# The input laid out by tiles, and Toeplitz blocks loaded in eighths over twelve groups

## The chip, the cores and the metric

The kernel runs on one core of a Trainium2 chip. The metric is the device time of one execution in microseconds. Before the change the median of three runs is 941.27 us (940.22 to 941.31).

## The reference

Two layers follow each other on x of shape 4 x 64 x 256 x 256 in float32. The first is a long two-dimensional convolution whose filter is separable: each channel has a filter hx along the rows and hy along the columns, both from a small network of sines.

```python
hx = _implicit_filter(z, Xw1, Xb1, Xw2, Xb2, Xw3, Xb3, Xwo, Xfreq, t, deltas)
hy = _implicit_filter(z, Yw1, Yb1, Yw2, Yb2, Yw3, Yb3, Ywo, Yfreq, t, deltas)
k = jnp.transpose(jnp.einsum('ijk,imk->ijmk', hx, hy)[0], (2, 0, 1))
k_f = jnp.fft.rfft2(k, s=(fft_size, fft_size)) / fft_size
u_f = jnp.fft.rfft2(x, s=(fft_size, fft_size))
y = jnp.fft.irfft2(u_f * k_f, s=(fft_size, fft_size))[..., :L, :L]
out = y + x * bias[:, None, None]
```

The second layer whitens the 64 channels: a mean and a covariance from every ninth pixel, five Newton-Schulz steps for its inverse square root, and a product with all pixels.

```python
x1_s = x1[:, ::STRIDE ** 2]
mean1 = jnp.mean(x1_s, axis=-1, keepdims=True)
cov = x1_s @ x1_s.T / x1_s.shape[1] + EPS * jnp.eye(B)
deconv = _isqrt_newton_schulz(cov, N_ITER)
out = deconv @ (x1 - mean1)
```

## The kernel before

**The start.** The filters are computed first (lines 134 to 163): four small matmuls deep, with sines on ScalarE and range reduction on VectorE between them. The result, `taps`, has 128 rows (64 channels of each of the two filters, f = 0 and f = 1) and 384 columns. It is stored to DRAM as `g_d` (line 166), and the two rows that the first channels need also as `g0_d` (line 165).

**Toeplitz blocks.** A convolution along one axis is a product with a Toeplitz matrix. `load_toeplitz` (line 173) makes that matrix by a DMA that reads `g_d` at addresses overlapping by one element from partition to partition. One set `toep[g]` serves a group g of eight channels: 128 partitions (two halves of 64), two filters, eight channels and 256 columns. There are eight sets, and two buffers for them. One call of `load_toeplitz` loads one half of the partitions of one filter, for all eight channels: 64 x 8 pieces of 1 KB, 512 KB. Four calls make a set.

**The main loop.** `steps` has 32 pairs (g, n): eight channel groups g, and for each the four images n. A step has four groups of work (`group`, line 302), each on two channels: c = 0, 2, 4, 6. So one g has sixteen groups, here counted as k = 4n + c/2. A group multiplies the two channels of x with the f = 0 Toeplitz blocks, which gives `o1`, and in the same stretch multiplies the `o1` made two groups earlier with the f = 1 blocks. `toeplitz_products` (line 185) splits both into blocks of 64 rows, so that one product runs on the upper and the other on the lower half of TensorE's rows at once. Each pair of 64-row block and filter half uses only the columns from its own offset on: line 208 takes `t[parts, : stop : -1]` with `stop = HP * k - 1`. For f = 0 the second half of the partitions (64 to 127) serves the odd blocks, and for f = 1 the first half does; odd blocks never use the first 64 columns.

**What follows a product.** ScalarE copies the first product to `o1` (line 320). VectorE adds x times the bias to the second and writes `y` (line 325), and it picks the sampled pixels for the covariance (line 249). SP stores y for the two channels to DRAM, `y_d` (line 339).

**The order on SP's queue.** The order of all engines in the main loop is that of the program text. SP issues, in each group: the store of y; then one load of x for two channels (`load_x`, line 103, 512 KB) of the step after next; then, in the four groups from c = 2 of n = 1 to c = 0 of n = 2, one quarter of the next Toeplitz set (lines 379 to 383). The store of y waits for VectorE, and what stands behind it on SP waits too. In x's place in DRAM a row of 256 pixels is 1 KB, and a tile's partition p takes the rows p and 128 + p of a channel, so that a load of x has 512 pieces of 1 KB.

**Before the loop.** SP issues the eight loads of x for the first two steps, then the store to `g0_d`, and then eight loads for `toep[0]` (lines 353 to 355): two channels of it first, from `g0_d`, and then the other six.

**The end.** From the step before the last on, SP reads y back in pieces of 2 MB (`yi`, line 287). After the covariance and the inverse root, TensorE multiplies, ScalarE and VectorE add the shift (lines 511 and 514), and GpSimd issues the stores of the output (line 519).

Of the kernel before, what the change touches and what calls it, by code (L numbers as in the profile page):

```python
# [44 lines left out]
NB, C, L = 4, 64, 256  # L45
P, H2 = 128, 2
EMB, ORDER = 33, 64
PIX = L * L
CG = 8
HP = P // 2  # L50
# [5 lines left out]
GW = P + L  # L56
# [9 lines left out]
def conv_whiten_kernel(ctx: ExitStack, tc: tile.TileContext, a: dict, out: bass.AP):  # L66
    nc = tc.nc
    x = a["x"]
# [28 lines left out]
    bias = const.tile([P, C], F32, tag="bias", name="bias")  # L97
    nc.scalar.dma_start(out=bias, in_=a["bias"].partition_broadcast(P))

    def new_x(g, n):  # L100
        return big.tile([P, CG, H2, L], F32, tag="in", name=f"x_{g}_{n}")

    def load_x(t, g, n, c):
        nc.sync.dma_start(
            out=t[:, c : c + 2].rearrange("p c b w -> p (c b) w"),
            in_=x[n, g * CG + c : g * CG + c + 2].rearrange("c (b p) w -> p (c b) w", p=P),
        )

    steps = [(g, n) for g in range(C // CG) for n in range(NB)]
    loaded = {s: new_x(*s) for s in steps[:2]}  # L110
    for step, t in loaded.items():
        for c in range(0, CG, 2):
            load_x(t, *step, c)

    ident = const.tile([P, P], F32, tag="ident", name="ident")
    make_identity(nc, ident)
# [1 line left out]
    for n in range(NB):  # L118
        t = spool.tile([P, FP], F32, tag="samp", name=f"samp{n}")
# [24 lines left out]
    for i in range(3):  # L144
        for u in range(2):
            pm = psA.tile([P, P], F32, tag="psA", name=f"pm{i}_{u}")
            nc.tensor.matmul(pm, lhsT=wt, rhs=hs[u], start=True, stop=True)  # L147
            half = slice(u * P, (u + 1) * P)
            arg, k, nxt = (scratch[:, 2 + 3 * i + v, half] for v in range(3))
# [9 lines left out]
    for u in range(2):  # L159
        half = slice(u * P, (u + 1) * P)  # L160
# [7 lines left out]
    def new_toeplitz(g):  # L168


        return tpool.tile([P, 2, CG, L], F32, tag="toep", name=f"toep_{g}")

    def load_toeplitz(t, g, f, half, lo=0, hi=CG):
        source, row = (g0_d, 2 * f) if g == 0 and hi == 2 else (g_d, f * C + g * CG + lo)
        nc.sync.dma_start(
            out=t[half * HP : (half + 1) * HP, f, lo:hi],
            in_=bass.AP(
                tensor=source.tensor,
                offset=source.offset + row * GW,
                ap=[[1, HP], [GW, hi - lo], [1, L]],  # L180
            ),
        )

# [41 lines left out]
    def pack_by_pe(g, n, yt, cs):  # L225

        pk = psA.tile([P, H2, cs.stop - cs.start, NJ], F32, tag="psA", name=f"pk_{cs.start}")
        for s in range(STEP):
            for b in range(H2):
                nj = (L - s + STEP - 1) // STEP  # L230
                nc.tensor.matmul(  # L231
                    pk[:, b, :, 0:nj],
                    lhsT=pick[:, (s - b) % STEP, :],
                    rhs=yt[:, cs, b, s : s + STEP * (nj - 1) + 1 : STEP],
                    start=(s == 0 and b == 0),
                    stop=(s == STEP - 1 and b == H2 - 1),
                    skip_group_check=True,
                )
        dst = samp[n][:, :, :, g * CG + cs.start : g * CG + cs.stop]
        nc.scalar.copy(dst[:, 0], pk[:, 0].rearrange("p c j -> p j c"))  # L240
        nc.vector.tensor_copy(dst[:, 1], pk[:, 1].rearrange("p c j -> p j c"))  # L241
# [15 lines left out]
    def covariance(n):  # L257

        pc = psA.tile([P, C + 1], F32, tag="psA", name=f"pc{n}")
        for b in range(H2):  # L260
            for j in range(NJ):
                half = slice(C * (j % 2), C * (j % 2 + 1))
                nc.tensor.matmul(  # L263
                    pc[half],
                    lhsT=samp[n][:, b, j, 0:C],
                    rhs=samp[n][:, b, j, :],
                    start=(b == 0 and j < 2),
                    stop=(b == H2 - 1 and j >= NJ - 2),
                    skip_group_check=True,
                )  # L270
        nc.vector.scalar_tensor_tensor(cov, pc, 1.0 / NSAMP, cov, ALU.mult, ALU.add)  # L271
# [18 lines left out]
    def load_next():  # L290
        loaded[len(loaded)] = load_y(len(loaded))

    loaded_x, loaded = loaded, {}
# [3 lines left out]
    def bank(name):  # L297
        return psA.tile([P, H2, L], F32, tag="psA", name=name)

    orders = [list(range(L // HP)), list(reversed(range(L // HP)))]  # L300

    def group(first, second):
# [46 lines left out]
    with tc.manual_schedule(  # L349
        engines={engines.PE, engines.SP, engines.DVE, engines.Activation, engines.Pool}  # L350
    ):
        toep = {0: new_toeplitz(0)}
        for lo, hi in ((0, 2), (2, CG)):
            for part in range(4):
                load_toeplitz(toep[0], 0, part // 2, part % 2, lo, hi)
        for i, (g, n) in enumerate(steps):
            xt = loaded_x.pop((g, n))
            yt = big.tile([P, CG, H2, L], F32, tag="out", name=f"y_{g}_{n}")
            for c in range(0, CG, 2):
                item = (g, n, c, xt, yt, [])  # L360
                if g == C // CG - 1 and n > 1 and c == 4:
                    covariance(n - 2)
                group(item, pending.pop(0) if len(pending) == 2 else None)
                pending.append(item)
                if i == 0 and c == 6:

                    fold = const.tile([P, C], F32, tag="fold", name="fold")
                    nc.vector.tensor_tensor(fold, ident[:, 0:C], ident[:, C:P], ALU.add)
                    twice = const.tile([C, 2, C], F32, tag="twice", name="twice")
                    for u in range(2):  # L370
                        nc.vector.tensor_copy(twice[:, u], ident[0:C, 0:C])

                part = (c - 2) // 2 % 4
                to = i + 2 if c else i + 1
                if to < len(steps) and to > 1:
                    if part == 0:
                        loaded_x[steps[to]] = new_x(*steps[to])
                    load_x(loaded_x[steps[to]], *steps[to], 2 * part)
                tg, tn = steps[i if c else i - 1]
                if tn == 1 and tg + 1 < C // CG and (i or c):  # L380
                    if part == 0:
                        toep[tg + 1] = new_toeplitz(tg + 1)
                    load_toeplitz(toep[tg + 1], tg + 1, part // 2, part % 2)
                if i + 2 >= len(steps) and c > 0:
                    for _ in range(2 if i + 2 == len(steps) and c == 2 else 1):
                        load_next()

        g, n, c, xt, yt, _ = pending[0]
        group(None, pending[0])
        pack_by_pe(g, n, yt, slice(0, CG // 2))  # L390
        group(None, pending[1])
        covariance(NB - 2)
        pack_by_pe(g, n, yt, slice(CG // 2, CG))
        covariance(NB - 1)
        while len(loaded) < len(homes):
            load_next()
# [3 lines left out]
    for i in range(2):  # L400
        t = o1pool.tile([P, H2 * L], F32, tag="o1", name=f"chain{i}")
# [90 lines left out]
    for i, (v, q) in enumerate(pieces):  # L492
# [3 lines left out]
        part = FP if 1 < i < len(pieces) - 2 else FP // 4  # L496
# [42 lines left out]
def _laid_out(inputs):  # L539

    import numpy as np

    def of(name):
        return [np.asarray(inputs[f"L0_conv_{f}{name}"]) for f in "XY"]

    zw = np.concatenate([np.asarray(inputs["L0_conv_z"])[0, ::-1].T] + of("w1"), axis=1)
    cols = np.stack([np.concatenate(of(k), axis=-1).reshape(P) for k in ("b1", "b2", "b3", "freq")], 1)
    wbd = np.zeros((P, 3, P), np.float32)
    for i, k in enumerate(("w2", "w3", "wo")):
        for f, w in enumerate(of(k)):  # L550
            wbd[f * ORDER : (f + 1) * ORDER, i, f * ORDER : (f + 1) * ORDER] = w
    return {"zw": zw, "cols": cols, "wbd": wbd.reshape(P, 3 * P)}
# [23 lines left out]
```

## Time and profile before

| | us |
|---|---|
| median of the runs | 941.27 |
| profiled execution | 938.56 |
| its span, first to last instruction | 936.8 |
| PE busy | 796.7 (85%) |
| PE weight loads busy | 639.0 (68%) |
| DVE busy | 649.5 (69%) |
| ACT busy | 480.7 (51%) |
| POOL busy | 31.7 (3%) |

The mean granted TensorE clock is 0.956. The page's last part lists the DMAs, with the median time from issue to landing:

```profile
x<-in_x_dram SPq DMA_DIRECT2D x128, 512.0 KB, 5.5
y_d<-y SPq DMA_DIRECT2D x128, 512.0 KB, 3.7
yi<-y_d SPq DMA_DIRECT2D x32, 2048.0 KB, 16.5
out_dram<-yi POOLq DMA_DIRECT2D x28, 2048.0 KB, 43.1
toep<-g_d SPq DMA_DIRECT2D x28, 512.0 KB, 10.3
```

PE is TensorE, DVE is VectorE, ACT is ScalarE, POOL is GpSimd and SP is the sync engine, which issues most of the DMAs. PEld is TensorE's loading of stationary operands, which overlaps its matmuls. The share of a DMA row is the mean busy share of the core's 16 DMA engines; it can read somewhat over 1. In the windows that follow, times are counted from the start of the span.

### The profile page before, as it was taken

To read this page: it belongs to the slowest core of one execution; us is meant where nothing else is said; L and a number is where in the kernel's file an instruction comes from. 1 tells how busy PE (TensorE), PEld (TensorE's weight loads), DVE (VectorE), ACT (ScalarE), POOL (GpSimd) and SP (SyncE) were. 2 spreads that over 40 slices of the span, in tenths; PEclk is the share of its full clock that TensorE was granted. 3 is DMA by queue.
4 is the path that set the end of the run, shared out by engine and by line. 5 is a ranking of instruction groups with operands and counts; after the bars stand their busy time and mean duration, and the time that the engine had idled before them with its cause. 6 is when DMAs were issued, how large, how long until landed. Compare 5 with 4: busy or idle time off the path is not lost.

```text
span 936.8 us, 27864 instructions
## 1 busy us (share of the span) xinstructions
PE 796.7 (85%) x11850; PEld 639.0 (68%) x11850; DVE 649.5 (69%) x861; ACT 480.7 (51%) x792; POOL 31.7 (3%) x71
## 2 busy tenths in 40 slices
PE   2999999999999999999999999999687777766400
PEld 2899999999999999899999999989421111111100
DVE  3058687778768786778687768662399999996600
ACT  2245454544445454445454545330299888876500
POOL 3000000000000000000000000000020000000010
PEclk9999999999999999999999999999799999998755
DMA  7499789779879879879979977899999999999998
GB/s 230 111 250 305 236 243 294 239 232 267 284 231 284 267 229 277 263 234 259 278 231 249 293 233 226 289 395 362 415 362 420 428 431 428 430 429 431 430 431 356
DMA packets 164112, 287.67 MB, mean 307 GB/s; under 512 B 6384, under 2 KB 154261, under 8 KB 156309
## 3 DMA queue, kind: packets, MB, share of 16 engines
q1 hardware_dynamic: 156784, 218.18, 72.3%
q0 software_dynamic: 6336, 67.11, 16.9%
q8 instruction: 94, 1.54, 0.7%
q10 hardware_dynamic: 868, 0.60, 0.2%
q14 instruction: 30, 0.24, 0.1%
HBM read 151.44 MB, written 134.42 MB: 305 GB/s over the span
## 4 chain that ended last, share of the span: by engine, by line
PE 69%; issue 15%; DVE 13%; DMA 1%; ACT 1%; POOL 0%; POOLq 0%; ACTq 0%; DVEq 0%; SPq 0%
PE p L205 65%; DVE yi L514 12%; PE pk L231 2%; PE pc L263 2%; POOL out_dram L519 0%; PE po L506 0%; DMA toep<-g_d 0%; DMA g_d<-scratch 0%; PE ZY L421 0%; DVE scratch L154 0%; PE YT L421 0%; PE pm L147 0%; DVE scratch L151 0%; ACT scratch L150 0%; ACT L439 0%
## 5 line engine op out<-in xcount | busy, mean ns | idle before, releaser
L205 PE MATMUL p<-toep,x 64*64 64x64 f32 (+3 forms) x5120 | 595.6, 287 | 8.0 <-DMA toep<-g_d 6.1
L205 PE MATMUL p<-toep,o 64*64 64x64 f32 (+3 forms) x5120 | 589.3, 285 | 1.3 <-issue 1.2
L205 PEld LDWEIGHTS p<-toep,x 64*128 64x128 f32 (+1 forms) x5120 | 546.3, 168 | 34.0 <-DMA toep<-g_d 6.3
L205 PEld LDWEIGHTS p<-toep,o 64*128 64x128 f32 (+1 forms) x5120 | 542.0, 166 | 13.7 <-issue 2.0
L320 ACT COPY o<-p 64x512 f32<-64x512 f32 x512 | 296.8, 580 | 318.3 <-PE p L205 310.7
L325 DVE SCALAR_TENSOR_TENSOR y<-x,bias,p 128x512 f32<-128x512 f32 x256 | 180.6, 743 | 169.1 <-PE p L205 168.2
L249 DVE COPY_PREDICATED samp<-mask,y 128x448 f32<-128x448 int32 (+1 forms) x279 | 275.5, 988 | 6.4
L514 DVE TENSOR_SCALAR yi<-po,shift 64x512 f32<-64x512 f32 x256 | 192.1, 750 | 22.5 <-PE po L506 15.9
L506 PE MATMUL po<-yi,W 64*64 64x512 f32 x1024 | 150.0, 654 | 62.6 <-DVE yi L514 41.3
L511 ACT ACTIVATE yi<-po,shift 64x512 f32<-64x512 f32 x256 | 174.8, 683 | 41.9 <-PE po L506 34.7
L506 PEld LDWEIGHTS po<-yi,W 64*64 64x64 f32 x1024 | 35.4, 141 | 176.3 <-DVE yi L514 128.7
L519 POOL DMA_DIRECT2D out_dram<-yi x44 | 23.6, 537 | 270.5 <-DMA out_dram<-yi 108.8
L405 POOL MEMSET chain<- 64x64 f32 x1 | 0.1, 144 | 618.6 <-PE p L205 618.6
L263 PEld LDWEIGHTS pc<-samp 128*64 128x64 f32 x464 | 14.3, 137 | 1.7 <-ACT samp L240 0.7
L231 PE MATMUL pk<-y,pick 128*128 128x112 f32 (+1 forms) x72 | 15.3, 386 | 0.0
L263 PE MATMUL pc<-samp 128*64 128x65 f32 x464 | 14.9, 223 | 0.4 <-ACT samp L240 0.4
L231 PEld LDWEIGHTS pk<-y,pick 128*128 128x128 f32 x72 | 14.5, 207 | 0.2
L240 ACT COPY samp<-pk 128x116 f32<-128x116 f32 x2 | 0.5, 270 | 25.8 <-PE pk L231 15.3
L147 PE MATMUL pm<-scratch 128*128 128x128 f32 (+1 forms) x12 | 3.8, 474 | 8.7 <-ACT scratch L156 6.2
L271 DVE SCALAR_TENSOR_TENSOR cov<-pc,cov 128x65 f32<-128x65 f32 x4 | 0.9, 228 | 12.1 <-PE pc L263 12.1
L147 PEld LDWEIGHTS pm<-scratch 128*128 128x128 f32 (+1 forms) x12 | 2.9, 313 | 9.4 <-ACT scratch L156 6.8
L241 DVE COPY samp<-pk 128x116 f32<-128x116 f32 x2 | 0.6, 279 | 11.4 <-ACT samp L240 11.4
(71 smaller groups left out, 46.7 us busy)
## 6 DMA issues: line engine op xcount, KB each, us to landing
x<-in_x_dram SPq DMA_DIRECT2D x128, 512.0 KB, 5.5
y_d<-y SPq DMA_DIRECT2D x128, 512.0 KB, 3.7
yi<-y_d SPq DMA_DIRECT2D x32, 2048.0 KB, 16.5
out_dram<-yi POOLq DMA_DIRECT2D x28, 2048.0 KB, 43.1
toep<-g_d SPq DMA_DIRECT2D x28, 512.0 KB, 10.3
out_dram<-yi POOLq DMA_DIRECT2D x16, 512.0 KB, 10.0
toep<-g_d SPq DMA_DIRECT2D x4, 384.0 KB, 7.6
toep<-g_d SPq DMA_DIRECT2D x4, 128.0 KB, 3.1
```

The source lines that it names most:

```text
L147: nc.tensor.matmul(pm, lhsT=wt, rhs=hs[u], start=True, stop=True)
L205: mm = nc.tensor.matmul(ps[q : q + w, m, HP * k : L], lhsT=src[parts, k // 2, m * P + q : m * P + q + w], rhs=t[parts, : stop : -1] if k e ...
L231: nc.tensor.matmul(pk[:, b, :, 0:nj], lhsT=pick[:, (s - b) % STEP, :], rhs=yt[:, cs, b, s : s + STEP * (nj - 1) + 1 : STEP], start=(s == 0 ...
L249: nc.vector.copy_predicated(dst, m, src)
L263: nc.tensor.matmul(pc[half], lhsT=samp[n][:, b, j, 0:C], rhs=samp[n][:, b, j, :], start=(b == 0 and j < 2), stop=(b == H2 - 1 and j >= NJ ...
L271: nc.vector.scalar_tensor_tensor(cov, pc, 1.0 / NSAMP, cov, ALU.mult, ALU.add)
L320: nc.scalar.copy(o1[to], units[u][0][0][fr])
L325: nc.vector.scalar_tensor_tensor(yt[:, c + u], xt[:, c + u], bias[:, ch : ch + 1], units[u][1][0], ALU.mult, ALU.add,)
L506: nc.tensor.matmul(po[u][halves[k]], lhsT=W[halves[u]], rhs=yt[halves[u], cols[k]], start=True, stop=True,)
L511: nc.scalar.activation(yt[halves[0], cols[k]], po[0][halves[k]], AF.Identity, bias=shift[halves[k]])
L514: nc.vector.tensor_scalar(yt[halves[1], cols[k]], po[1][halves[k]], shift[halves[k]], None, ALU.add)
L519: nc.gpsimd.dma_start(out=o[:, end - part : end], in_=yt[:, end - part : end])
```

## The change

The change has four parts.

1. The host hands x over in the order of the tiles: image, channel group, partition, channel, row half, pixel. A load of x then reads 4 KB that lie together for each partition, 128 pieces instead of 512.
2. Before the loop only the first step's x is loaded. The four loads of the second step's x are issued behind the eight loads of `toep[0]`.
3. The next Toeplitz set is loaded in eighths (four channels instead of eight), in the groups k = 2, 3, 5, 6, 8, 10, 11 and 13 of the g before it. The first set keeps its eight loads.
4. In half of the Toeplitz loads (where filter and half differ) the first 64 columns, which no product reads, are left out: 768 B in a piece instead of 1 KB.

```diff
     def load_x(t, g, n, c):
         nc.sync.dma_start(
-            out=t[:, c : c + 2].rearrange("p c b w -> p (c b) w"),
-            in_=x[n, g * CG + c : g * CG + c + 2].rearrange("c (b p) w -> p (c b) w", p=P),
+            out=t[:, c : c + 2],
+            in_=x[n, g][:, c : c + 2],
         )
...
-    for step, t in loaded.items():
-        for c in range(0, CG, 2):
-            load_x(t, *step, c)
+    for c in range(0, CG, 2):
+        load_x(loaded[steps[0]], *steps[0], c)
...
     def load_toeplitz(t, g, f, half, lo=0, hi=CG):
         source, row = (g0_d, 2 * f) if g == 0 and hi == 2 else (g_d, f * C + g * CG + lo)
+        skip = 0 if f == half else HP
         nc.sync.dma_start(
-            out=t[half * HP : (half + 1) * HP, f, lo:hi],
+            out=t[half * HP : (half + 1) * HP, f, lo:hi, skip:],
             in_=bass.AP(
                 tensor=source.tensor,
-                offset=source.offset + row * GW,
-                ap=[[1, HP], [GW, hi - lo], [1, L]],
+                offset=source.offset + row * GW + skip,
+                ap=[[1, HP], [GW, hi - lo], [1, L - skip]],
             ),
         )
...
+    spread = [2, 3, 5, 6, 8, 10, 11, 13]
...
             for part in range(4):
                 load_toeplitz(toep[0], 0, part // 2, part % 2, lo, hi)
+        for c in range(0, CG, 2):
+            load_x(loaded_x[steps[1]], *steps[1], c)
...
-                tg, tn = steps[i if c else i - 1]
-                if tn == 1 and tg + 1 < C // CG and (i or c):
+                k = 4 * n + c // 2
+                if k in spread and g + 1 < C // CG:
+                    part = spread.index(k)
                     if part == 0:
-                        toep[tg + 1] = new_toeplitz(tg + 1)
-                    load_toeplitz(toep[tg + 1], tg + 1, part // 2, part % 2)
+                        toep[g + 1] = new_toeplitz(g + 1)
+                    lo = part % 2 * CG // 2
+                    load_toeplitz(
+                        toep[g + 1], g + 1, part // 4, part // 2 % 2, lo, lo + CG // 2
+                    )
...
+    x = np.asarray(inputs["x"]).reshape(NB, C // CG, CG, H2, P, L).transpose(0, 1, 4, 2, 3, 5)
+    given = {"x": x, "bias": inputs["L0_conv_bias"], **_laid_out(inputs)}
```

More of the change, by code (lines that the diff above doesn't have):

```diff
@@ L558 @@
     from concourse.bass_utils import run_bass_kernel_spmd
-    given = {"x": inputs["x"], "bias": inputs["L0_conv_bias"], **_laid_out(inputs)}
+    x = np.asarray(inputs["x"]).reshape(NB, C // CG, CG, H2, P, L).transpose(0, 1, 4, 2, 3, 5)
+    given = {"x": x, "bias": inputs["L0_conv_bias"], **_laid_out(inputs)}
     given.update(_constants())
```

## The prediction

> **What bounds the kernel now.** I read the page's slices first, then windows, then the chain of waits, then SP's timeline.
>
> ```profile
> PE   2999999999999999999999999999687777766400
> ...
> DMA  7499789779879879879979977899999999999998
> GB/s 230 111 250 305 236 243 294 239 232 267 284 231 284 267 229 277 263 234 259 278 231 249 293 233 226 289 395 362 415 362 420 428 431 428 430 429 431 430 431 356
> ...
> q8 instruction: 94, 1.54, 0.7%
> ```
>
> There are two stages. Up to about 660 us PE is full (the convolution). After that DMA is full at 430 GB/s (the 67 MB of y read back and 67 MB of output). The change touches only loads of the first stage and leaves PE, DVE, ACT and POOL with the same instructions in the same order, so it can pay only where PE waits, or runs late, for a load. The second stage begins when the convolution lets it, with the same bytes, so what the first stage gains or loses passes through to the end one to one. The same windows for DMA:
>
> ```profile
> 11.00:16.00 5.00, 2.53 (x8) 1.92 (x8) 2.88 (x13) 2.00 (x6) 3.52 (x7) 1.00 1.10 358
> 96.00:105.13 9.13, 9.13 (x164) 8.59 (x162) 7.33 (x9) 4.64 (x8) 0.00 (x0) 1.00 0.74 228
> ...
> 356.00:376.00 20.00, 20.00 (x347) 18.91 (x347) 15.74 (x20) 10.71 (x19) 0.00 (x0) 1.00 1.12 278
> 376.00:378.00 2.00, 0.88 (x11) 0.56 (x9) 1.63 (x2) 0.00 (x0) 0.00 (x0) 1.00 1.09 373
> ```
>
> Columns: window, its length, busy us of PE, PEld, DVE, ACT, POOL, PE clock, DMA share, GB/s. Two quiet groups (96 to 105) use DMA to 0.74; while a Toeplitz set loads (issued 352.5 to 367) and for some ten microseconds after, the share is 1.12: full, with a backlog. At the end of that stretch PE stands still, with the clock at 1.00. The chain of waits calls these stops "issue", so nothing in the program holds PE there:
>
> ```profile
> 376.34 1.12 issue
> 377.45 72.44 PE p L205 x1252
> 449.90 0.55 issue
> 450.45 9.64 PE p L205 x160
> ```
>
> A third, 0.68 us, is at 515.62. The three Toeplitz sets before them are issued at 352.5 to 367, 427 to 442 and 502 to 517. Since PE's instructions themselves arrive by DMA (q8: 94 packets of 16 KB; of the span's 27,864 instructions PE and PEld have 23,700), the natural reading is a page of instructions held up behind the backlog. SP's timeline gives the full size, since every group of matmuls ends in one store of y:
>
> ```profile
> 369.79 0.87 SPq L339 DMA_DIRECT2D y_d<-y  x1
> ...
> 374.72 0.37 SPq L339 DMA_DIRECT2D y_d<-y  x1
> ...
> 380.48 0.37 SPq L339 DMA_DIRECT2D y_d<-y  x1
> ```
>
> Here one interval is 5.76 us; in its place in a quiet stretch it is 4.3. Four quiet intervals make 18.3 us, so sixteen (one g) make 73.2. The seven sums of sixteen from the first store (44.28) are 73.16, 73.55, 73.48, 73.67, 74.88, 74.64 and 74.33: **5.3 us more than 7 x 73.2**. The long intervals lie in or just behind the Toeplitz loads. Of the 5.3, 2.35 us (1.12 + 0.55 + 0.68) is PE visibly idle; the rest is late weight loads (PEld waits for "issue" 3.4 us between 35 and 592) and small slips.
>
> **The change part by part.**
>
> *DMA load of a group.* Before, quiet: 0.74 x 9.13 / 2 = 3.38 us of full share. Of it x is 0.524 MB at the 358 GB/s of the 11 to 16 us window, 1.46 us x 1.10 = 1.61; so the y store is 1.77. A Toeplitz quarter: the window 130 to 162, share 1.06, moves 0.32 x 32 = 10.2 us more than a quiet one, for four quarters: 2.5 us each. So a loading group asks 3.38 + 2.5 = 5.9 us, and 4.57 us at share 1.1 gives 5.0: the backlog.
>
> *After.* An eighth is half of a quarter, 1.25 us; where 64 columns are left out it has 25% fewer bytes but as many pieces, so between 0.94 and 1.25. I take 1.25. For x, pieces of 4 KB replace 1 KB. [...] The rows say 358 GB/s for x in 1 KB pieces at share 1.10, and 430 at share 1.01 for the second stage, whose pieces are 16 KB: 0.524 MB / 430 = 1.22 us. [...]
>
> *The stalls.* With no backlog the 5.3 us should mostly go: between 2.35 (only the visible idle time) and 5.3. I take 4.5, because the quiet stretches too have DMA in flight and late pages need not vanish. [...] The row shows PE idle with nothing to wait for, three times out of three at the tail of a saturated stretch, so I go by the row.
>
> *More issues.* 28 more DMAs on SP at 0.59 to 1.05 us are 16 to 29 us, hidden: SP's work in a loading group is 0.37 + 0.54 + 1.05 = 2 of 4.57 us, then it waits for DVE to make the next y. [...] But completion is waited for by nobody near: the f = 0 half is issued by k = 6, nine groups (41 us) ahead of its use, the f = 1 half by k = 13, four groups (18 us of cover) ahead of the next g's k = 2, against landings of 7.1 to 14.3 us for whole quarters. Cost 0; if cover failed, one landing less 18 us.
>
> *The added early wait.* The first eighth, at k = 2, takes the buffer that PE last reads at k = 1. It stands on SP behind the y store of k = 2, which waits for DVE on products of k = 2, so the buffer is already free: 0. Behind it is the next y store, over 4 us later.
>
> *The start.*
>
> ```profile
> 16.45 0.26 SPq L165 DMA_DIRECT2D g_d<-scratch  x1
> 16.98 0.36 ACTq L166 DMA_DIRECT2D g_d<-scratch  x1
> 18.84 5.30 SPq L175 DMA_DIRECT2D toep<-g_d  x8
> 22.09 15.12 PE L205 MATMUL p<-toep,x 64*128 64x256 f32 x79 [6.05 <-DMA toep<-g_d]
> ```
>
> The filter's chain sets this, not x: taps ready 16.4, stored and landed 18.8, reloaded 22.1. The 4 MB of x run until about 17 us, so with 2 MB (5.9 us at 358 GB/s) the store loses a neighbour for its first half microsecond. DMA is empty from 19 to 20, so the reload had none. Gain 0 to 0.6; I take 0.3. The second x tile, now behind the eight Toeplitz loads on SP, has issue at about 24 us; those loads are over at 33 before, x adds 5.9: landed by 39, and needed at about 46 by the fifth group. Cost 0, with 7 us in hand; the first y store on SP is at 44.
>
> *Sum* against the profiled 938.56 (span 936.8 and 1.8 around it): 4.5 + 0.3 = 4.8, so 933.8. The median of the runs shown is 941.27, 0.3% above the profiled execution; I take the same 4.8 from it: **936.5 us**.
>
> **Rivals.**
>
> *No change: the pages are late of their own accord.* For it: three of seven sets show clear stops and the first three hardly any excess (0 to 0.35). Against: every stop lies at the tail of a saturated stretch. Only the start remains: 941.0. Chance 0.17.
>
> *Slower: longer pieces hold the engines.* With 4 KB pieces and Toeplitz loads over twelve groups, a page may meet a busy engine anywhere. From 597 to 632, beside 16 KB pieces at share 1.02, PE stops once, 0.66 us in 35: 0.019. Over 550 us of convolution that would be 10.4, less 4.8: 946.9. It decides from a rate of 4.8 / 550 = 0.009 on. Against: x is in flight for only 1.2 of 4.57 us, and in its pieces only a quarter as long as those. Chance 0.10.
>
> *Only the visible stops go*: 2.35 + 0.3, 938.6; or more than the sum goes, since the unprofiled runs are 2 to 3 us longer and may hold more stops: 933. Both belong to the forecast's own case, chance 0.73.
>
> **How the numbers follow.** A measurement here can tell about 0.2%, 1.9 us, from no change: faster means below 939.4. The forecast's case gives nearly all of faster, 0.72; same 0.16; slower 0.12. The range goes from 933, the whole excess with more in the unprofiled runs, to 941.5, which takes in the case of no change.
>
> **What would show it.** The DMA share stays below 1.05 through the convolution, quiet groups fall to about 0.65, and the backlog stretches are gone. "Issue" leaves the chain between 40 and 592, and each sum of sixteen y stores is 73.2 to 73.6. First matmul at 21.5 to 22.1. The x loads land in less than 5.5 us. The covariance, the inverse root and the output stage keep their lengths. It is wrong if the stops remain while DMA is no longer full, if the groups' own pace of 18.3 us for four moves, or if the output stage changes its length.

## The result and the profile after

The changed kernel takes 933.67 us (median of four runs, 931.3 to 935.08), beside 941.29 us before (four runs, 940.22 to 943.36). The ratio is 0.9914, with a 95% interval of 0.9887 to 0.9941: 0.6 to 1.1% faster. The forecast was 936.5, within 933.0 to 941.5. The profiled execution took 931.3 us (span 929.4), 7.3 less than the one of before.

First the page of the changed kernel: the slices of PE and DMA, the queue of instructions, and the DMA issues with the median time to landing.

```profile
PE   3999999999999999999999999999787777765500
...
DMA  4698888888888988888878887899999999999998
...
q8 instruction: 94, 1.54, 0.7%
...
x<-in_x_dram SPq DMA_DIRECT2D x128, 512.0 KB, 5.6
y_d<-y SPq DMA_DIRECT2D x128, 512.0 KB, 4.0
...
toep<-g_d SPq DMA_DIRECT2D x28, 256.0 KB, 6.1
toep<-g_d SPq DMA_DIRECT2D x28, 192.0 KB, 5.9
```

The row of DMA is even now: 8 in most slices of the convolution, where before it went up and down between 7 and 9. PE's row is as full as it was, since the time that went away was never visible in tenths of a slice. Loads of x land no sooner than before (5.6 us, against 5.5). The windows show the stretch in which PE stood still before (columns as in the prediction, the last two are DMA share and GB/s):

```profile
356.00:376.00 20.00, 20.00 (x340) 18.74 (x338) 15.69 (x20) 10.11 (x18) 0.00 (x0) 1.00 0.84 252
376.00:378.00 2.00, 2.00 (x24) 1.84 (x22) 1.97 (x4) 1.49 (x3) 0.00 (x0) 1.00 0.88 290
```

The share is 0.84 where it was 1.12, and PE works through. The chain of waits of the changed kernel, asked for 40 to 590 us, has no "issue" left:

```profile
39.94 546.67 PE p L207 x9555
586.62 3.41 PE pc L265 x110
```

**Where the time came from.** SP's stores of y divide the span. The 7.3 us of span that the two profiles differ by are: 1.25 up to the first store (44.28 before, 43.03 after), 4.99 in the next 112 groups (517.71 before, 512.72 after; the seven sums of sixteen are now 73.15 to 73.31), and 1.10 behind them. Only the middle part returned when the changed kernel was profiled again (e9 below): there the first store is at 43.94, the 112 groups take 512.98, and the rest takes 374.7 us against 374.8 before. So of the two profiles' difference some 5 us belong to the change. The rest is within what the start and the end vary by over the fourteen profiles of this document (first store at 42.8 to 45.4, 373.7 to 377.0 us behind the 112 groups).

### The profile page after: what moved, and what is told of

It reads as the page before. It is cut to its first block, busy times and chain, and to the rows that moved or that the text cites. A ratio compares the mean times of both kernels' runs of the same rounds, so it can differ in the third digit from the quotient of the medians.

```text
span 929.4 us, 27874 instructions
## 1 busy us (share of the span) xinstructions
PE 793.8 (85%) x11850; PEld 636.4 (68%) x11850; DVE 648.4 (70%) x861; ACT 481.1 (52%) x792; POOL 31.8 (3%) x71
## 3 DMA queue, kind: packets, MB, share of 16 engines
q8 instruction: 94, 1.54, 0.7%
## 4 chain that ended last, share of the span: by engine, by line
PE 69%; issue 15%; DVE 13%; ACT 1%; POOL 0%; DMA 0%; POOLq 0%; DVEq 0%; ACTq 0%; SPq 0%
PE p L207 65%; DVE yi L524 12%; PE pk L233 2%; PE pc L265 2%; POOL out_dram L529 0%; DMA toep<-g_d 0%; PE po L516 0%; PE ZY L431 0%; PE YT L431 0%; DVE scratch L153 0%; PE pm L146 0%; ACT scratch L149 0%; PE pf L161 0%; DVE scratch L150 0%; ACT L449 0%
## 5 line engine op out<-in xcount | busy, mean ns | idle before, releaser
L524 DVE TENSOR_SCALAR yi<-po,shift 64x512 f32<-64x512 f32 x256 | 192.1, 750 | 22.1 <-PE po L516 15.8
```

Of the source, the lines that this page charges most:

```text
L524: nc.vector.tensor_scalar(yt[halves[1], cols[k]], po[1][halves[k]], shift[halves[k]], None, ALU.add)
```

## The experiments

All twelve kernels were timed in five rounds beside the kernel before, in three sessions: e1 to e4, e5 to e8, e9 to e12. The kernel before had medians of 942.81, 943.90 and 942.16 us in them, so kernels of different sessions are compared by their ratios. "112 groups" is the time in each one's profile from the first y store to the 113th. "Stops" is the time in which PE waited for "issue" between 40 and 590 us of that profile. "Pages late" says when the packets of the instruction queue q8 begin, compared with the changed kernel at the same place among the groups, as a mean over k = 6 to 12. Each profile is one execution, and not always a middling one: those of before and e2 are among the fastest of their runs, that of e8 is the slowest of six.

| kernel | median us | ratio to before, 95% interval | 112 groups us | stops us | pages late us |
|---|---|---|---|---|---|
| before, profiled once | 938.56 profiled | | 517.71 | 2.4 | 2.5 |
| changed | 933.67 | 0.9914 (0.9887 to 0.9941) | 512.72 | 0 | reference |
| e1 spread alone | 933.92 | 0.9906 (0.9879 to 0.9932) | 512.98 | 0 | -0.1 |
| e2 layout alone | 947.06 | 1.0047 (1.0030 to 1.0065) | 520.95 | 5.3 | 2.8 |
| e3 late x alone | 945.04 | 1.0019 (1.0001 to 1.0036) | 523.55 | 7.9 | 2.7 |
| e4 skip alone | 939.18 | 0.9970 (0.9952 to 0.9987) | 516.55 | 1.8 | 2.2 |
| e5 all but the spread | 943.64 | 0.9992 (0.9971 to 1.0012) | 519.78 | 4.0 | 2.4 |
| e6 spread and more loads | 937.91 | 0.9942 (0.9925 to 0.9960) | 517.89 | 2.8 | 2.3 |
| e7 eighths in a row | 939.26 | 0.9956 (0.9940 to 0.9972) | 517.91 | 1.9 | 2.1 |
| e8 quarters apart | 934.76 | 0.9901 (0.9874 to 0.9928) | 515.21 | 0.8 | 1.0 |
| e9 changed again | 933.59 | 0.9912 (0.9886 to 0.9938) | 512.98 | 0 | -0.2 |
| e10 spread, late x, skip | 933.11 | 0.9905 (0.9882 to 0.9928) | 512.98 | 0 | |
| e11 spread, skip | 933.82 | 0.9913 (0.9890 to 0.9936) | 513.02 | 0 | |
| e12 layout and more loads | 936.73 | 0.9943 (0.9926 to 0.9960) | 516.65 | 2.5 | 2.0 |

### Each part alone

The first question was which of the four parts does it.

**e1, the spread alone:** the new rule of loading (k in `spread`, eighths), with everything else as before.

```diff
-                tg, tn = steps[i if c else i - 1]
-                if tn == 1 and tg + 1 < C // CG and (i or c):
...
+                k = 4 * n + c // 2
+                if k in spread and g + 1 < C // CG:
```

> Before, with the Toeplitz eighths over twelve groups alone; x as before, all 256 columns loaded, both first x tiles loaded at the start. Backlog theory (pages of instructions come late behind a full DMA queue): the 112 groups from the first y store take 512.7 to 513.5 us instead of 517.7, no stop of PE by issue in them, the start stays at 22.1 for the first matmul, and the time falls by 5 to 6 us, to about 935.5. If the layout of x is what cures the backlog, the stops stay and the 112 groups take 516 or more.

Measured: 933.92 us, no stop, 112 groups in 512.98. That is the whole gain of the change, and the 112 groups are as the backlog theory said; the time fell by 8.9 us against the median of before, more than the 5 to 6 expected. The other three parts are not needed for it. The DMA engines carry the same load as before on average, first in the kernel before and then in e1:

```profile
40.00:590.00 550.00, 547.65 (x9559) 515.65 (x9558) 411.76 (x500) 275.44 (x476) 0.00 (x0) 1.00 0.87 254
```

```profile
40.00:590.00 550.00, 550.00 (x9675) 517.29 (x9673) 414.38 (x504) 278.26 (x480) 0.00 (x0) 1.00 0.87 257
```

The share is 0.87 in both; only its distribution in time differs.

**e2, the layout of x alone:**

```diff
-            in_=x[n, g * CG + c : g * CG + c + 2].rearrange("c (b p) w -> p (c b) w", p=P),
+            in_=x[n, g][:, c : c + 2],
```

> Before, with x laid out by the host in 4 KB pieces alone. By the forecast's sum (x costs 1.23 instead of 1.61 us of DMA a group) the backlog grows by half as much, the 112 groups take about 515 us and the time falls by 2 to 3 us. By the quiet groups of the changed kernel, which use no less DMA than before (3.68 against 3.45 us of full share a group), x is no cheaper in 4 KB pieces: 112 groups at 517 to 519, and the time within 1.5 us of before.

Measured: slower, by 0.3 to 0.65%, which neither expectation had, though the second was right about the DMA: two quiet groups ask as much of it as before. Here is the window of e2; the same window of before had 0.74 and 228 GB/s.

```profile
96.00:105.13 9.13, 9.13 (x164) 8.59 (x163) 6.45 (x8) 4.65 (x8) 0.00 (x0) 1.00 0.76 233
```

Over the three quiet groups from k = 15 to 1, as a mean of six g, it is 3.43 us of full share a group before and 3.45 in e2. So x in pieces of 4 KB is not cheaper. In e2's chain of waits the stops are longer than before:

```profile
235.39 142.76 PE p L205 x2498
378.15 2.82 issue
380.97 71.88 PE p L205 x1253
452.85 0.88 issue
```

**e3, the second x tile late, alone:**

```diff
-    for step, t in loaded.items():
-        for c in range(0, CG, 2):
-            load_x(t, *step, c)
+    for c in range(0, CG, 2):
+        load_x(loaded[steps[0]], *steps[0], c)
...
+        for c in range(0, CG, 2):
+            load_x(loaded_x[steps[1]], *steps[1], c)
```

> Before, with the second x tile loaded behind the eight Toeplitz loads alone. If the store of the taps waited behind x on the queue, it lands in about 1.2 us instead of 2.3, the first matmul is at 20.6 to 21.0 instead of 22.1, the first y store at 43.0 to 43.3, and the time falls by 1.0 to 1.5 us; the 112 groups stay at 517.7. By the forecast's 0.3 us the first matmul is at 21.8.

Measured: the first matmul is at 20.83, as the larger expectation said, and the first y store at 42.79, a little before it. But the kernel as a whole is slower, if only just (1.0001 to 1.0036), and its profile holds more stops than any other. The gain of the start also proved to be no property of this part: e1, e2 and e4, which load both x tiles first, start at 20.75 to 20.98 too. This is taken up below.

**e4, the 64 columns left out, alone:**

```diff
+        skip = 0 if f == half else HP
...
-                ap=[[1, HP], [GW, hi - lo], [1, L]],
+                ap=[[1, HP], [GW, hi - lo], [1, L - skip]],
```

> Before, with the 64 unread columns left out alone. If a Toeplitz load costs by its pieces, nothing changes: 112 groups at 517.7, time within 1 us. If by its bytes, half the loads cost a quarter less, a loading group asks 5.6 instead of 5.9 us of DMA against 5.0 to be had, the backlog shrinks by a third and the 112 groups take about 516 us, 1.5 to 2 us off the time.

Measured: 0.2 to 0.5% faster, 112 groups in 516.55. The second expectation, that a load costs by its bytes, had the direction; by the medians 3.6 us go, where it said 1.5 to 2. One profile with 1.8 us of stops against 2.4 is too little to show that the stops shrank with the bytes.

### Is it the spread, and is it the backlog

**e5, everything but the spread:** the changed kernel with the old rule for quarters in four groups in a row.

> The changed kernel with the Toeplitz loads back in quarters in four groups in a row: x in 4 KB pieces, second x tile late, 64 columns left out. Backlog theory: the stops are back, the 112 groups take 516 to 521 us (layout alone took 520.95, the skip alone 516.55), pages of instructions come 2 to 5 us late behind the Toeplitz loads, and the time is 940 to 946, no better than before. If layout, late x and skip together bring something, it is under 938.

Measured: 943.64, ratio 0.9992 (0.9971 to 1.0012). The profile has 4.0 us of stops, and the 112 groups take 519.78, both as the backlog theory said. Without the spread nothing of the gain is left.

**e6, the spread with other loads:** e1 with four more loads of x in the groups k = 4 to 7. Nothing reads them.

```diff
+                if n == 1 and g + 1 < C // CG:
+                    load_x(spare_x, g, n, c)
```

> e1_spread with four more loads of x for two channels (512 KB each, into a tile that nothing reads until it is overwritten) in the groups k = 4 to 7 of each g, so that DMA has a backlog again without the Toeplitz loads in a row; it computes the same. Backlog theory: a group asks about 3.4 + 1.6 + 0.6 to 1.2 = 5.6 to 6.2 us of DMA against 5.0, stops come back at k = 6 to 11, the 112 groups take 515 to 523, the time is 937 to 946. If the Toeplitz loads themselves (their overlapping, unaligned reads) hold up the pages, the 112 groups stay at 513 and the time at 934.

Measured: the stops are back with Toeplitz loads spread out. The larger two lie in the group k = 9, behind the added loads; in all kernels with stops the larger ones lie in k = 9 to 11. These are windows of e6 and a piece of its chain of waits:

```profile
356.00:376.00 20.00, 20.00 (x384) 18.84 (x375) 15.78 (x20) 10.91 (x19) 0.00 (x0) 1.00 1.10 310
496.00:516.00 20.00, 20.00 (x363) 18.63 (x354) 15.79 (x20) 10.95 (x20) 0.00 (x0) 1.00 1.07 293
```

```profile
450.85 65.22 PE p L205 x1122
516.07 1.06 issue
517.14 72.93 PE p L205 x1269
```

The share is 1.10 and 1.07, and PE stops at 516.07. So added loads of x do it as well, and Toeplitz loads in a row are not needed. The loss does not follow the amount of DMA work: over the twelve groups from k = 2 to 13, e6 asks 4.73 us of full share a group and the kernel before 4.34, but the ratio of e6 (0.9942) puts it only 3.4 us above e1, where the kernel before lies 8.9 above. Why it loses less is open.

**e7, eighths in a row:** each quarter is issued as two eighths in the same four groups.

```diff
-                    load_toeplitz(toep[tg + 1], tg + 1, part // 2, part % 2)
+                    for lo in (0, CG // 2):
+                        load_toeplitz(toep[tg + 1], tg + 1, part // 2, part % 2, lo, lo + CG // 2)
```

> Before, with each Toeplitz quarter issued as two eighths in the same four groups. Backlog theory: same bytes in the same groups, same backlog, 112 groups at 517 to 521, time within 3 us of before. If smaller DMAs help by themselves (a page then waits behind less), the 112 groups fall below 515.

Measured: the profile is as the backlog theory said (517.91, one stop of 1.8 us, share 1.11 from 356 to 376). The time is not: 939.26, ratio 0.9940 to 0.9972, 4.6 us below before where 3 was the limit. Smaller DMAs in the same groups bring about half of the gain. The other expectation had that direction, but put it into the 112 groups (below 515). Why is not known. The profile also shows a second loss, in e7 alone. Right behind the stop, which ends at 379.05, the granted clock is halved for 3.4 us:

```profile
379.40:382.80 3.40, 3.40 (x20) 2.71 (x18) 0.75 (x1) 1.16 (x2) 0.00 (x0) 0.50 0.94 329
```

At half the clock 3.4 us do the work of 1.7, an estimate from the share of 0.50. So the stop and the halved clock together cost about 3.5 us, and not 1.8: the sum of sixteen groups in which they lie is 77.19 us, against the quiet 73.2. Without the halved clock the 112 groups of this profile would take some 516.2 us, an estimate from these numbers.

**e8, quarters apart:** whole quarters at k = 2, 5, 8 and 11.

```diff
+                k = 4 * n + c // 2
+                if k in (2, 5, 8, 11) and g + 1 < C // CG:
+                    part = (k - 2) // 3
```

> Before, with whole quarters in the groups k = 2, 5, 8 and 11 instead of four in a row. Backlog theory: a loading group leaves 0.9 us of DMA work behind, the two quiet groups after it have 1.6 us each to spare, so no backlog lasts: no or few stops, 112 groups at 513 to 514, time 934 to 936, nearly all of the gain without eighths. If eighths are needed, 112 groups stay above 515.

Measured: 934.76, with ratio 0.9901, and 0.8 us of stops. Nearly the whole gain comes with four loads per set and no eighths, if two quiet groups lie between them. The 112 groups take 515.21, over the expected 513 to 514; the profile is that of the slowest run (937.22), and pages are still a microsecond late in it.

### What stops PE

"Issue" in a chain of waits only says that the profile shows no releaser. The packets of q8 point to one. This is the DMA view of the kernel before, for the window from 447.5 to 448 us, in which one packet of 16 KB begins:

```profile
q1 hardware_dynamic: 118, 0.11, 111.0%
q8 instruction: 1, 0.02, 17.7%
```

The packet meets 16 engines that are already full with q1. It begins at 447.60; PE stops at 449.90 and goes on at 450.45, 2.85 us after this packet began. The other two stops of before end 2.85 and 2.83 us after a packet (374.61 to 377.45, 513.48 to 516.31). Over nine kernels with stops there are 24 of 0.5 us or more between 40 and 592 us, and **every one ends 2.3 to 3.1 us after a packet of q8 begins**, while such packets come about every 7 us; by chance one end in nine would.

A second count points to the page itself. The profile of before has 24,127 instructions of TensorE (weight loads, matmuls and 427 of its sequencer) and 94 packets of q8, so about 256 (256.7) to a packet. At the ends of the three stops of before, 12,225, 14,785 and 17,089 of them have begun: 10 and 9 times 256 apart. In all nine kernels the number at the end of a stop leaves the same remainder, 193, when it is divided by 256, at the 24 stops and at the 20 shorter ones. PE stops at one and the same place of a packet's worth of instructions, and nowhere else.

From these counts it is concluded that the packets hold TensorE's instructions and that PE waits for the next page of them. The page is late because it began late: the packet itself takes a median of 1.07 us before and 1.19 in the changed kernel. In the kernel before the pages between k = 6 and 12 begin 2.5 us later on average than in the changed kernel at the same place, and up to 5.3 us; in all other places, 0.5 us earlier. There is little room for this. In the five profiles without stops a page begins 5.8 to 6.1 us (median) before the instruction at which a stop would end, and in none of the fourteen more than 8.1 us, about one page ahead. By these figures a delay of some 3 us uses that up, and the stop is what is left of it. When a page is asked for, the profile does not show; that it waits in line behind data is concluded from the backlog.

The backlog can be counted too: the bytes that SP has issued, less those whose packets on q1 have begun. Over the 112 groups its peak is 1.35 to 1.45 MB in the five profiles without stops, 1.63 in e8, and 2.10 to 2.65 in the other eight. A single full group did no harm: in e1 the share of a group reaches 1.10. But no more than two groups in a row reach 0.98 there, in the other profiles without stops and in e8, while in the other eight it is five to twelve.

### Together, and what is best

The changed kernel again, and two kernels that leave parts of it out.

> The changed kernel once more, beside the next two: 932 to 935, 112 groups at 512.7 to 513.3, first y store between 42.8 and 44 (its taps land in 1.2 to 1.3 us, as in all three runs so far with the second x tile late).

> The changed kernel with x in its old place in DRAM (1 KB pieces). If the layout brings nothing once the backlog is gone, it stays within 1 us of e9; if the 4 KB pieces, which made the kernel of before slower (e2_layout), cost here too, it is 1 to 3 us faster than e9, the fastest so far; by the forecast's cheaper x it is slower than e9.

> e1_spread with the 64 columns left out: within 1 us of e1_spread (933.9), since no stops are left to remove: 112 groups at 512.7 to 513.3. Against e10 it shows the late second x tile: by the landing of the taps (1.2 us with it, 1.25 to 2.6 without) e10 should be about 0.5 us faster.

Measured: 933.59, 933.11 and 933.82 us. The three, the first measurement of the changed kernel and e1 lie within 0.8 us, and the intervals of their ratios overlap widely. Once the backlog is gone, the layout, the late x and the skip bring nothing that can be told from nothing, and cost nothing either. There is no version here that clearly beats the changed kernel; e1 is as fast with one part of four. The windows from 40 to 590 us of e9 (x in 4 KB pieces) and of e10 (1 KB) bear this out:

```profile
40.00:590.00 550.00, 550.00 (x9658) 517.29 (x9657) 414.30 (x504) 278.26 (x480) 0.00 (x0) 1.00 0.82 253
```

```profile
40.00:590.00 550.00, 550.00 (x9674) 517.29 (x9672) 414.32 (x504) 278.27 (x480) 0.00 (x0) 1.00 0.84 254
```

PE is busy for all 550 us in both; the layout saves at most 0.02 of share, some 0.1 us a group.

**e12, longer pieces in a backlog:** e6 with x in the new layout.

> e6_spread_and_load with x, and so the added loads too, in 4 KB pieces. If longer pieces make a page of instructions wait longer in a backlog (as e2_layout suggests), it is slower than e6 (937.9) by 2 to 5 us; if e2's loss has another cause, it is within 1.5 us of e6 or faster.

Measured: 936.73, no slower than e6. By the ratios the two are equal (0.9943 and 0.9942). So long pieces do not make a backlog worse as such, and the loss in e2 stays unexplained.

## Why the prediction was right

**The bound and the path of the gain: right.** PE sets the first stage, and the second only moved: in the 255 us from 674 before and from 667 after, DVE works 192.25 and 192.26 us, and DMA moves 421 GB/s in both.

**The mechanism: right, by all that the traces show.** The stops were pages of instructions that began 2.5 us late on average (k = 6 to 12) behind a DMA backlog. The forecast inferred this from where the stops lay. The packets of q8 and the count by 256 point to the page, e1 against e5 shows that the spread of the loads decides, and e6 shows it from the other side. The signs named for it came: no group of the changed kernel has a DMA share over 1.04, "issue" is gone from the chain, and the sums of sixteen are at 73.2 to 73.3. The quiet groups and the landing of x (5.6 us, forecast under 5.5) did not follow the forecast; that is the matter of x below.

**The stops at 4.5 us: right for the profile, too small for the usual run.** The profiles give 4.99 and, in e9, 4.73. The medians give 7.6 to 9.1, between 933.1 and 933.9 for the kernels without stops and 941.3 to 942.8 for the kernel before beside them. The step that was mis-sized is "I take the same 4.8 from it": the working came from a profiled execution of 938.56 us, and the runs of before reach from 938.42 to 949.27. The kernels without stops reach only from 931.3 to 935.44. So it is likely the stops that make the runs of before differ, and that its profile showed an execution with few of them. Other kernels' profiles of that length do have more: e2, e3 and e5, profiled at 941.34 to 943.76, hold 4.0 to 7.9 us of stops. No profile of a run of before of median length was taken. The forecast had named this as the reason why more might go.

**x in 4 KB pieces: wrong.** The row of 430 GB/s put x at 1.22 (1.23 in what was expected of e2) instead of 1.61 us a group. Measured, a quiet group asks 3.43 us without the new layout and 3.45 with it (before and e2): here pieces of 1 and of 4 KB cost the same. The row was the wrong one: it came from a stage of other loads and stores, in which all 16 engines were full (share 1.01). The quiet groups were to fall to a share of 0.65 and stayed at 0.80 (changed) and 0.77 (e9; four groups from k = 14), against 0.74 before. The error cost nothing. By the forecast's own figures a loading group asks 1.77 + 1.22 + 1.25 = 4.24 us with x at 1.22, and 4.63 with x at 1.61. These estimates from the rows of before are both below the 5.0 us to be had.

**An eighth at 1.25 us, or 0.94 with columns left out: a little high.** With 3.45 as the quiet group, the twelve groups from k = 2 to 13 ask 4.17 us each in e1, which makes (4.17 - 3.45) x 12 / 8 = 1.08 for an eighth, and 3.98 in e11, which makes 0.80 as a mean over full and short ones. With the quiet groups of these kernels themselves (3.54 and 3.48) it is 0.95 and 0.75.

**The start at 0.3 us: of the right size, and lost in chance.** The first matmul is at 20.64 in the changed kernel and 20.70 in e9, earlier than the forecast's 21.5 to 22.1, but it is at 20.20 to 20.98 in five kernels with both x tiles loaded first, too. The store of the taps is issued at 15.9 to 16.5 in all kernels. The first reload follows 1.22 to 1.29 us later in the five profiles with the second x tile late, and 1.25 to 2.58 us later in the nine without (mean 1.69): waiting behind x costs up to 1.3 us, and often nothing. SP's timeline of e7 and e9:

```profile
16.55 0.26 SPq L165 DMA_DIRECT2D g_d<-scratch  x1
19.13 5.30 SPq L175 DMA_DIRECT2D toep<-g_d  x8
```

```profile
16.32 0.26 SPq L164 DMA_DIRECT2D g_d<-scratch  x1
17.55 5.30 SPq L177 DMA_DIRECT2D toep<-g_d  x8
```

The mean saving is 0.45 us. Between e10 and e11, which differ only in this, the medians differ by 0.7, less than the runs of either spread.

**Hidden costs at 0: right.** With 28 more DMAs on SP and the first eighth at k = 2, no matmul between 40 and 590 us waits for a Toeplitz block or for x.

**The rivals.** "No change: the pages are late of their own accord" is ruled out by e1, in which the spread alone takes the stops away, and e5, in which they are back without it. "Longer pieces hold the engines" did happen where a backlog was left: e2 is 0.5% slower. It had no hold on the changed kernel, which keeps the backlog from lasting. In e6 against e12 the same pieces did no harm, so its mechanism is not confirmed. Why e3, which moves one transfer near the start, shows stops of 1.9 us as late as 307 us, is open too; its interval only just excludes no change.

## What to carry to other kernels

Where an engine stops for "issue" in an unrolled kernel, look at what the DMA queues did in the 10 us before: here 94 packets of q8 (1.54 MB of instructions) went beside the data, and in the eight profiles with a backlog of 2.10 MB or more they began 2.0 to 2.8 us late (k = 6 to 12), though no matmul between 40 and 590 us waited for a load. Spread loads that have much time over more of it, so that the DMA engines catch up after each; a single full group of 4.6 us did no harm here, five or more in a row did, at the same average share of 0.87. A small gain forecast from one profiled execution is set against the spread of the runs: those of before reach from 938.42 to 949.27 us, those of the kernels without stops from 931.3 to 935.44.

## What was not expected of the hardware

TensorE's rate in the first groups is a source of chance of its own. In all profiles the matmuls over 256 columns last 0.63 us at first and 0.38 us from some moment on. This is the timeline of PE in the kernel before:

```profile
38.71 0.63 PE L205 MATMUL p<-toep,x 64*128 64x256 f32 x1
38.88 0.55 PE L205 MATMUL p<-toep,o 64*128 64x256 f32 x1
39.14 0.42 PE L205 MATMUL p<-toep,x 64*128 64x256 f32 x1
39.27 0.38 PE L205 MATMUL p<-toep,o 64*128 64x256 f32 x1
```

The traces point to the clock. The windows print 1.00 for this stretch too, but the trace holds no record of the clock there: the first record, of the full clock, begins at 39.2 in this kernel, and within 0.1 us of the first matmul at the fast rate in all fourteen profiles. In the 3.4 us of e7 in which a clock of 0.50 is on record, the same matmuls last 0.63 us again.

The step comes 17 us after the first matmul (22.09), when both halves of the rows have worked at once for 2.7 us. In the changed kernel it came at 38.2; in e9, with the first matmul within 0.1 us of the same moment, at 40.0. Over all kernels it comes 16.6 to 19.6 us after the first matmul and 2.1 to 5.1 us after both halves began to work at once. From the first matmul to the first y store it is 21.9 us where the step comes earliest and 23.4 where it comes latest: half of the difference between 16.6 and 19.6 us, as half the rate would have it. In the timeline of before the products of x begin 0.43 us apart up to the step (38.71, 39.14) and 0.22 us apart behind it (39.40, 39.62). The 1.5 us between 21.9 and 23.4 are more than the 0.3 us that the late x tile was to save. What sets the moment of the step was not tested.
